# A graph network's max aggregation: eleven tiles taken with one product per pair of source tiles instead of one per source tile

## The chip, the cores and the metric

The kernel runs on one core of one Trainium2 chip. The metric is the device time of one execution in microseconds; the time before is 3248.2 us, the median of three runs (3247.44, 3248.2, 3262.78). Engines are named as the profile names them: PE multiplies matrices, PEld loads its weights, DVE, ACT and POOL are the vector, scalar and GpSimd engines, SP issues most DMAs.

## The reference, cut to what matters

Three layers of a graph network over 6250 nodes and 200,000 edges, sorted by destination. Destinations are drawn as 6250 u² with u uniform, so low-numbered nodes have many edges and high ones few (about 58 a node in tile 3, 33 in tile 11, 24 in tile 21, 20 in tile 30).

```python
def _sage_conv(x, src, dst, Wl, bl, Wr):
    agg = jax.ops.segment_max(x[src], dst, num_segments=x.shape[0])
    agg = jnp.where(jnp.isfinite(agg), agg, 0.0)
    return agg @ Wl + bl + x @ Wr
...
h = jax.nn.leaky_relu(_sage_conv(x, src, dst, Wl1, bl1, Wr1), NEG_SLOPE)
h = jax.nn.leaky_relu(_sage_conv(h, src, dst, Wl2, bl2, Wr2), NEG_SLOPE)
h = jax.nn.leaky_relu(_sage_conv(h, src, dst, Wl3, bl3, Wr3), NEG_SLOPE)
...
h = jnp.maximum(_layernorm(x, axis=-1), 0.0)
x = x + _L0_gnn_ref(h, edge_index, L0_gnn_Wl1, ...)
```

The first layer has 128 features, the second and third 256 on their input side.

## The kernel before, in words

**Tiles.** Nodes are cut into 50 tiles of 127; tile numbers serve for sources and destinations. The 50 source tiles form 25 pairs g. For a tile of destinations and a pair of source tiles, the kernel makes a *one-hot* matrix (in `one_hot`): column d has a one in the row of one source of destination d. The product of the pair's features (`pair_sb`, in two parts whose sum is exact) and the one-hot picks that source's features for all destinations of the tile, and DVE takes the maximum into the accumulator `acc` (`maxima`, L1007). A destination can have several sources in a pair; those that a product does not pick go on a *list* and are fetched row by row.

**Units.** A unit is 128 columns of a one-hot. A *wide* unit ("w") picks one source per source *tile*: two products a pair, each with a maximum of its own. A *narrow* unit ("n") picks one source per *pair*: the products with both source tiles (s = 0 and 1) add up in one PSUM tile `pg`, and one maximum takes it. Both kinds cost PE the same matmuls. Before, tiles 3 to 21 are wide and 22 to 49 narrow; tiles 0 to 2, with the most edges, are spread over eight "virtual" wide units and eight more ("x") that are handled as narrow.

**Groups and sweeps.** Group 0 holds the narrow tiles 30 to 49, group 1 the virtual units, group 2 the wide tiles 3 to 21, group 3 the narrow tiles 22 to 29. A *sweep* runs over all 25 pairs, from the last to the first, for some groups: in layer 0 the groups 0, then 1, then 2 and 3 (called 0a, 0b, 0c here); in layer 1 the groups 0 and 1, then 2 and 3 (1a, 1b); in layer 2 the groups 0 and 1, then 2, then 3 (2a, 2b, 2c). One *step* of the program is one chunk of up to 1024 columns (512 in layers 1 and 2) of one group and pair: eight matmuls of L990 (four where a chunk of layer 0 is at most 512 wide) and one maximum (narrow) or two (wide). There are 225 + 400 + 400 steps.

**Lists.** Each group has a list. `CAPS` gives, for each row of 128 destinations (sorted by how much they have listed), how many gathers it gets; a destination with more than its cap sends the program through a slow fallback behind a branch at the end. The caps sum to 118 + 70 + 230 + 77 = 495 gathers a layer. One gather is an indirect DMA issued by POOL (`Listed.gather`, L1039) that fetches 128 rows of `table` into a quarter (an eighth in layer 0) of a tile `g`; its addresses `let` are copied by ACT from `ell` two steps ahead (`release`, L1028); DVE merges a full `g` into the first (L1053) and folds the result (L1058).

**What sets the order.** The order is written out by hand. `plan(step, rank, f)` puts each gather, release, maximum and node update at a step; gathers are spread evenly over a layer's steps, and their maxima come DELAY = 8, 6, 6 steps later (SOON = 4 for list 3). Each engine runs its own queue in that order, so an engine that is late delays whoever waits for it, and ACT, which makes the one-hots as buffers come free, goes in step with PE.

**Nodes.** When a group is done, `Node` fetches its listed maxima (POOL, L1082), merges them with `acc` (L1098, L1104), does the linear part (L1109 to L1115), and writes the next layer's tables, pairs and transposed rows. The 20 nodes of group 0 and the joined ones of group 1 fall into the first 50 steps of the following sweep, the nodes of groups 2 and 3 into the first 27 steps of the next layer.

**Chores.** The lists and one-hot indices of groups 1 to 3 are made on DVE while layer 0 runs: `flag_rows` finds repeated sources (L488 to L548), `pick_rows` picks what is listed with rounds of MAX8 and MATCH_REPLACE (L558, L560), `rank_rows` sorts, `send_row` scatters by POOL (L624), and `expand` with `lookups` make the index rows (L736 to L769). Group 1's stand in steps 0 to 40, those of groups 2 and 3 in steps 40 to 82. A wide tile needs two look-ups (s = 0 and 1) over 64 columns, a narrow one a single look-up over 40.

Of the kernel before, what the change touches and what calls it, by code (L numbers as in the profile page):

```python
# [36 lines left out]
I16 = mybir.dt.int16  # L37
# [22 lines left out]
)  # L60
NEAR, FIRST = 20, 30
DEEP = (24, 24, 48, 24)
# [7 lines left out]
def kernel(ctx: ExitStack, tc: tile.TileContext, x, src, dst,  # L70
# [31 lines left out]
    PLACE, HEAD = {}, []  # L102
    for units in GROUPS:
        HEAD.append(len(PLACE))
        for u in units:
            PLACE[u] = len(PLACE)
    NU = len(PLACE)
# [4 lines left out]

    TILES = [[tile_of(u) for u in units] for units in GROUPS]
    LISTS = GROUPS
# [30 lines left out]
    IW = [(len(units) + sum(w == "w" for w, _ in units)) * P for units in PLANES]  # L145
# [3 lines left out]
    OW = [sum(w == "w" for w, _ in units) * P for units in PLANES]  # L149
# [400 lines left out]
    def pick_rows(k, i0, us, S):  # L550

        n, W, m = len(us), width_of(us), DEEP[k]
# [10 lines left out]
        nc.vector.tensor_scalar(picked[k][:, i0 : i0 + n, :], top, -float(LEAF), 0.0, op0=OP.add, op1=OP.max)  # L563
        there = S(0, F32, n, m)
        nc.vector.tensor_scalar(there, top, float(LEAF), None, op0=OP.is_ge)
        nc.vector.reduce_sum(left_n[k][:, i0 : i0 + n], there, axis=AX.X)
# [183 lines left out]
    def lookups(us, least, s, pool, tags=("v", "v8")):  # L750
# [9 lines left out]
        while i < n:  # L760
# [9 lines left out]
            at = NV + PLANES[k].index(us[i]) if us[i] in EXTRA else GROUPS[k].index(us[i]) + (len(GROUPS[k]) if s else 0)  # L770
# [61 lines left out]
    for i0 in (0, NEAR // 2):  # L832
        mask_rows(L0[i0 : i0 + NEAR // 2], S_first)
        flag_rows(L0[i0 : i0 + NEAR // 2], S_first)
# [6 lines left out]
        pick_rows(0, i0, L0[i0 : i0 + NEAR // 2], S_first)  # L841
# [88 lines left out]
    def parts_of(k):  # L930

        units = PLANES[k]
        for w in "wnx":
            us = [i for i, u in enumerate(units) if u[0] == w]
            for i0 in range(0, len(us), HOT // P):
                yield us[i0], len(us[i0 : i0 + HOT // P]) * P, len(GROUPS[k]) if w == "w" else 0
# [3 lines left out]
    def one_hot(layer, k, g, c, w, odd, s):  # L940
# [7 lines left out]
        if layer == 0:  # L948
            at = of + (c + (odd if s else 0) + (NV if PLANES[k][c] in EXTRA else 0)) * P
# [27 lines left out]
    def products(step, s, p):  # L977
# [4 lines left out]
        c0, pw, _ = next(q for q in parts_of(k) if q[0] <= c < q[0] + q[1] // P)  # L982
# [82 lines left out]
    class Node:  # L1065
# [28 lines left out]
        def merge(self):  # L1094
# [5 lines left out]
            if self.k is None:  # L1100
# [171 lines left out]
    for layer in range(3):  # L1272
# [7 lines left out]
        for part, t0, t1 in (((lists_[:3], t0, turn), (lists_[3:], turn, t1)) if alone else ((lists_, t0, t1),)):  # L1280
# [3 lines left out]
            n = sum(len(li.seq) for li in part) - early  # L1284
# [6 lines left out]
        done_at, i, at = [], 0, 0  # L1291
        for k, li in enumerate(lists_):
            for t in range(len(li.seq)):
                if whens[i] is None:
                    at = 1 + i // 8
                else:
# [447 lines left out]
```

## Time and profile before

| | us |
|---|---|
| median of three runs | 3248.2 |
| profiled execution, device time | 3258.48 |
| its span, first to last instruction | 3256.5 |

The page has one slice for each fortieth of the span. Its rows on PE, DVE, POOL and the clock:

```profile
PE   1025622448777779999988888889999997878787
DVE  6677899987999987899986799995799897999965
POOL 4787523446777742766664455532466665654563
PEclk9996865678999999999999999999999998999999
```

A digit is the busy share of a slice in tenths; PEclk is the granted clock of TensorE in tenths of full speed. The first three slices are the preparation before the first product. A row of a view by line reads: line, engine, operation, output and input, shapes, count | busy us, mean ns of one | idle us just before them and what ended it. A row of waits reads: who waited, for whom, us in total, times, longest.

### The profile page before, as it was taken

To read this page: it belongs to the slowest core of one execution; us is meant where nothing else is said; L and a number is where in the kernel's file an instruction comes from. 1 tells how busy PE (TensorE), PEld (TensorE's weight loads), DVE (VectorE), ACT (ScalarE), POOL (GpSimd) and SP (SyncE) were. 2 spreads that over 40 slices of the span, in tenths; PEclk is the share of its full clock that TensorE was granted. 3 is DMA by queue.
4 is the path that set the end of the run, shared out by engine and by line. 5 is a ranking of instruction groups with operands and counts; after the bars stand their busy time and mean duration, and the time that the engine had idled before them with its cause. 6 is when DMAs were issued, how large, how long until landed. Compare 5 with 4: busy or idle time off the path is not lost.

```text
span 3256.5 us, 37116 instructions
## 1 busy us (share of the span) xinstructions
PE 2448.4 (75%) x9919; PEld 1785.3 (55%) x9920; DVE 2740.2 (84%) x4320; ACT 1901.7 (58%) x2753; POOL 1862.4 (57%) x1885
## 2 busy tenths in 40 slices
PE   1025622448777779999988888889999997878787
PEld 1023311235444457777765655567777775655566
DVE  6677899987999987899986799995799897999965
ACT  4127942646867656666654566655666664555553
POOL 4787523446777742766664455532466665654563
PEclk9996865678999999999999999999999998999999
DMA  9234521339866767666766655656666575655586
GB/s 305 59 66 139 150 68 33 110 99 242 241 185 194 183 189 230 199 208 201 204 167 192 203 165 177 171 154 212 206 197 203 180 179 181 201 166 159 155 258 182
DMA packets 358250, 571.20 MB, mean 175 GB/s; under 512 B 65270, under 2 KB 213379, under 8 KB 357393
## 3 DMA queue, kind: packets, MB, share of 16 engines
q1 hardware_dynamic: 237201, 341.17, 32.7%
q0 software_dynamic: 77568, 193.35, 23.6%
q10 hardware_dynamic: 43264, 34.21, 3.2%
q8 instruction: 83, 1.36, 0.2%
q14 instruction: 134, 1.10, 0.1%
HBM read 443.95 MB, written 124.54 MB: 175 GB/s over the span
## 4 chain that ended last, share of the span: by engine, by line
PE 36%; DVE 29%; DMA 12%; issue 9%; POOL 5%; ACT 4%; SPq 1%; DVEq 0%; ACTq 0%; POOLq 0%
PE pg L990 28%; DVE acc L1007 13%; POOL g L1039 5%; DMA g<-table,let 4%; PE z_p L1111 3%; DVE g L1058 3%; PE z_p L1113 2%; DVE g L1053 2%; ACT hot L962 2%; ACT away L960 2%; DMA pair_sb<-pair 2%; DVE acc L742 1%; DVE acc L560 1%; DVE acc L558 1%; DVE acc L736 1%
## 5 line engine op out<-in xcount | busy, mean ns | idle before, releaser
L990 PE MATMUL pg<-hot,pair_sb 128*128 128x512 f32 (+1 forms) x8000 | 2150.7, 417 | 411.2 <-ACT hot L962 126.4
L1039 POOL DMA_INDIRECT g<-table,let x1485 | 1510.7, 1017 | 929.1 <-ACT let L1028 359.9
L990 PEld LDWEIGHTS pg<-hot,pair_sb 128*128 128x128 f32 x8000 | 1507.6, 199 | 925.8 <-ACT hot L962 236.8
L1007 DVE TENSOR_TENSOR acc<-acc,pg 128x1024 f32<-128x1024 f32 (+3 forms) x1439 | 1638.3, 1166 | 278.4 <-PE pg L990 251.3
L962 ACT ACTIVATE hot<-away 128x1024 fp32r<-128x1024 uint8 (+2 forms) x600 | 573.9, 957 | 405.8 <-PE pg L990 391.8
L962 ACT ACTIVATE hot<-idx_sb 128x1024 fp32r<-128x1024 uint8 (+2 forms) x600 | 555.0, 937 | 230.3 <-PE pg L990 216.0
L960 ACT ACTIVATE away<-idx_sb,near 128x1024 uint8<-128x1024 uint8 (+2 forms) x600 | 620.4, 1034 | 56.7 <-DMA idx_sb<-idx 25.8
L1082 POOL DMA_INDIRECT agg<-best,end_i x141 | 141.1, 1001 | 236.2 <-PE aT_p L1098 190.6
L1115 ACT COPY s<-z_p 127x256 f32<-127x256 f32 (+1 forms) x150 | 50.3, 335 | 308.1 <-PE z_p L1113 258.4
L1053 DVE TENSOR_TENSOR g<-g 128x1024 f32<-128x1024 f32 (+5 forms) x211 | 206.6, 979 | 10.8 <-DMA g<-table,let 10.7
L1058 DVE TENSOR_TENSOR g<-g 128x256 f32<-128x256 f32 (+3 forms) x357 | 175.5, 492 | 10.6 <-DVE g L1053 0.2
L1111 PE MATMUL z_p<-wr,hT_in 128*128 128x256 f32 (+1 forms) x500 | 136.3, 390 | 1.0 <-DMA hT_in<-across 0.9
L1028 ACT ACTIVATE let<-ell 128x4 int32<-128x4 int16 (+3 forms) x435 | 78.5, 190 | 92.8 <-DMA ell<-picks 82.6
L1113 PE MATMUL z_p<-wl,mz 128*128 128x256 f32 (+1 forms) x500 | 119.7, 356 | 12.2 <-DVE mz L1104 11.4
L624 POOL DMA_INDIRECT picks<-picked,to_i x55 | 56.8, 1032 | 120.9 <-DVE rank_h L600 90.4
L1104 DVE TENSOR_TENSOR mz<-acc,aT_p 128x256 f32<-128x256 f32 (+1 forms) x141 | 52.5, 372 | 72.7 <-PE aT_p L1098 72.7
L956 DVE TENSOR_SCALAR hot<-idx_sb,beyond 128x1024 fp32r<-128x1024 uint8 (+1 forms) x150 | 108.5, 723 | 0.0
L1113 PEld LDWEIGHTS z_p<-wl,mz 128*128 128x128 f32 x500 | 88.6, 203 | 23.8 <-DVE mz L1104 13.8
L1111 PEld LDWEIGHTS z_p<-wr,hT_in 128*128 128x128 f32 x500 | 80.9, 204 | 33.8 <-issue 11.5
L867 ACT COPY hT<-hT_p 128x254 f32<-128x254 f32 x100 | 36.9, 369 | 80.5 <-PE hT_p L865 80.4
L354 POOL DMA_INDIRECT win_d<-in_dst_dram,win_i x50 | 54.2, 1084 | 46.6 <-ACT junk_w L359 18.0
L767 PE MATMUL lk_p<-ident_b,v 128*25 128x128 bf16 x90 | 10.5, 285 | 87.9 <-DVE v L755 59.4
(281 smaller groups left out, 1212.6 us busy)
## 6 DMA issues: line engine op xcount, KB each, us to landing
pair_sb<-pair SPq DMA_DIRECT2D x325, 256.0 KB
idx_sb<-far SPq DMA_DIRECT2D x50, 640.0 KB
far<-away ACTq DMA_DIRECT2D x225, 128.0 KB
pair<-pr SPq DMA_DIRECT2D x100, 256.0 KB
g<-table,let POOLq DMA_INDIRECT x1485
idx_sb<-idx SPq DMA_DIRECT2D x25, 608.0 KB
idx_sb<-far SPq DMA_DIRECT2D x50, 304.0 KB
idx_sb<-idx SPq DMA_DIRECT2D x50, 304.0 KB
```

The source lines that it names most:

```text
L956: nc.vector.tensor_scalar(hot[:, :w], d, beyond, None, op0=OP.is_equal)
L960: nc.scalar.activation(away, d, AF.Abs, bias=near[:, s : s + 1], scale=1.0)
L962: nc.scalar.activation(hot[:, :w], d, AF.Relu, bias=1.0, scale=-1.0)
L990: nc.tensor.matmul(to, pr[:, i, kk * P : (kk + 1) * P], hot[:, o : o + bw], start=((alone or s == 0) and i == 0), stop=((alone or s == 1) ...
L1007: nc.vector.tensor_max(to, to, of)
L1028: nc.scalar.activation(let[:, :n], ell[self.k][:, q, j : j + n], AF.Identity, scale=1.0)
L1039: nc.gpsimd.indirect_dma_start(out=self.tiles[q, b][:, i, :], out_offset=None, in_=tables[self.layer], in_offset=bass.IndirectOffsetOnAxis ...
L1053: nc.vector.tensor_max(base[:, : i + 1, :], base[:, : i + 1, :], g[:, : i + 1, :])
L1058: nc.vector.tensor_max(base[:, :h, :], base[:, :h, :], base[:, w - h : w, :])
L1082: nc.gpsimd.indirect_dma_start(out=self.agg[:, : self.F], out_offset=None, in_=of, in_offset=bass.IndirectOffsetOnAxis(ap=at, axis=0),)
L1111: nc.tensor.matmul(z_p, self.hT[:, i, :], wr[layer][:, i, :], start=False, stop=False)
L1113: nc.tensor.matmul(z_p, self.m[:, i, :], wl[layer][:, i, :], start=False, stop=(i == K - 1))
```

## The change

The border between wide and narrow moves from tile 22 to tile 11: `HI = 11`. Tiles 11 to 21 become narrow: one look-up of 40 columns in place of two of 64, one maximum a pair in place of two, and everything else that their destinations have in a pair is listed. The groups are cut anew: group 2 is the wide tiles 3 to 10 and the narrow tiles 18 to 29 (20 units for 19), group 3 the narrow tiles 11 to 17 (7 for 8). The caps become 118 + 70 + 255 + 110 = 553 gathers a layer. `pick_rows` takes fewer rounds for the narrow tiles of group 2 (32 of 48 places, `NARROWLY`) and the list of group 3 gets 40 places. In layer 2, whose last sweep is group 3 alone, the first 34 gathers of list 3 now come ahead of list 2's, with the usual delay; the other 76 stand in the end as all 77 did. The number of steps is the same, as are matmuls per step but for widths.

```diff
 CAPS = (
     (22, 10, 9, 8, 8, 7, 6, 6, 6, 5, 5, 4, 4, 4, 3, 3, 3, 2, 2, 1),
     (21, 12, 10, 9, 7, 5, 4, 2),
-    (47, 24, 20, 17, 15, 13, 12, 11, 10, 9, 8, 8, 7, 6, 6, 5, 5, 4, 3),
-    (23, 12, 10, 9, 7, 6, 5, 5),
+    (47, 25, 21, 18, 16, 14, 13, 12, 11, 11, 10, 9, 8, 8, 7, 7, 6, 5, 4, 3),
+    (34, 18, 15, 13, 12, 10, 8),
 )
-NEAR, FIRST = 20, 30
-DEEP = (24, 24, 48, 24)
+NEAR, FIRST, MID, HI = 20, 30, 18, 11
+LISTED = 0
+NP = NEAR - LISTED
+DEEP = (24, 24, 48, 40)
+NARROWLY = (24, 0, 32, 40)
...
-    WIDE = list(range(VT, 22))
-    NARROW = list(range(FIRST, NT)) + list(range(22, FIRST))
+    WIDE = list(range(VT, HI))
+    NARROW = list(range(FIRST, NT)) + list(range(MID, FIRST)) + list(range(HI, MID))
     NW, NN = len(WIDE), len(NARROW)
+    BOTH = NEAR + FIRST - MID
     GROUPS = (
-        [("n", i) for i in range(NEAR)],
+        [("n", i) for i in range(NP)],
         [("w", NW + v) for v in range(NV)],
-        [("w", i) for i in range(NW)],
-        [("n", i) for i in range(NEAR, NN)],
+        [("w", i) for i in range(NW)] + [("n", i) for i in range(NEAR, BOTH)],
+        [("n", i) for i in range(BOTH, NN)],
     )
...
     def pick_rows(k, i0, us, S):
 
-        n, W, m = len(us), width_of(us), DEEP[k]
+        n, W, most = len(us), width_of(us), DEEP[k]
+        m = min(most, NARROWLY[k]) if us[0][0] == "n" else most
...
+        if m < most:
+            nc.vector.memset(picked[k][:, i0 : i0 + n, m:], 0)
+            full = S(0, F32, n, 1)[:, :, 0]
+            nc.vector.tensor_scalar(full, left, float(m), float(most - m), op0=OP.is_ge, op1=OP.mult)
+            nc.vector.tensor_add(left, left, full)
...
-        for part in [us]:
+        for part in [list(p) for _, p in itertools.groupby(us, key=lambda u: u[0])]:
             chores.append((2.5, lambda part=part: mask_rows(part, S_acc)))
-            chores.append((18 if part[0][0] == "w" else 6, lambda part=part: flag_rows(part, S_acc)))
+            chores.append((len(part) * (1 if part[0][0] == "w" else .6), lambda part=part: flag_rows(part, S_acc)))
...
-    for i0, i1 in ((0, 7), (7, 13), (13, 19)):
-        for s in range(2):
-            late_lookups(LISTS[2][i0:i1], s)
+    for s in range(2):
+        late_lookups(LISTS[2][:NW], s)
+    rest2 = LISTS[2][NW:]
+    cuts = -(-len(rest2) // 8)
+    for i in range(cuts):
+        late_lookups(rest2[len(rest2) * i // cuts : len(rest2) * (i + 1) // cuts], 0)
...
+        items = [(k, t) for k in range(NL) for t in range(len(lists_[k].seq))]
+        if alone:
+            own = [(3, t) for t in range(len(lists_[3].seq))]
+            later_n = len(items) * (t1 - turn) / (t1 - t0)
+            heads = [t for t, (_, j) in enumerate(lists_[3].seq) if j == 0]
+            cut = min(heads, key=lambda t: abs(len(own) - t - later_n))
+            mid = next(i for i, (k, _) in enumerate(items) if k == 2)
+            items = items[:mid] + own[:cut] + [q for q in items if q[0] == 2] + own[cut:]
+            parted = len(items) - (len(own) - cut)
...
```

DVE's queue in sweep 2b (layer 2, group 2). L1007 is the accumulator maximum, 128x2x512 for a chunk of four units; L1053 and L1058 merge and fold gathered rows. Before, some two pairs:

```order
L1007 TENSOR_TENSOR acc_1513<-acc_1513,pg 128x2x512 x7
L1007 TENSOR_TENSOR acc_1513<-acc_1513,pg 128x2x384 x2
L1007 TENSOR_TENSOR acc_1513<-acc_1513,pg 128x2x512
L1053 TENSOR_TENSOR g<-g 128x1024
L1007 TENSOR_TENSOR acc_1513<-acc_1513,pg 128x2x512 x4
L1053 TENSOR_TENSOR g<-g 128x512
L1058 TENSOR_TENSOR g<-g 128x512
L1058 TENSOR_TENSOR g<-g 128x256
L1007 TENSOR_TENSOR acc_1513<-acc_1513,pg 128x2x512 x3
L1007 TENSOR_TENSOR acc_1513<-acc_1513,pg 128x2x384 x2
```

Now, at the same place (the lines have moved by seven):

```order
L1014 TENSOR_TENSOR acc_1514<-acc_1514,pg 128x2x512 x8
L1060 TENSOR_TENSOR g<-g 128x1024
L1014 TENSOR_TENSOR acc_1514<-acc_1514,pg 128x2x512 x2
L1060 TENSOR_TENSOR g<-g 128x512
L1065 TENSOR_TENSOR g<-g 128x512
L1065 TENSOR_TENSOR g<-g 128x256
L1014 TENSOR_TENSOR acc_1514<-acc_1514,pg 128x2x512 x7
```

A pair had eight 512-wide and two 384-wide maxima; it has seven 512-wide ones. The folds of gathered rows stand closer together.

POOL's queue from sweep 0c over the border of the layers into 1a. L1039 is the gather (table_75 is layer 0's table, table_76 layer 1's), L1082 a node's fetch. Before:

```order
L1039 DMA g<-table_75,let 128x128 x159
L1082 DMA agg<-best_2_142,end_i_852 128x128 x19
L1082 DMA agg<-best_3_143,end_i_853 128x128 x8
L1039 DMA g<-table_76,let 128x256 x252
L1082 DMA agg<-best_0_144,end_i_850 128x256
```

Now:

```order
L1046 DMA g<-table_75,let 128x128 x179
L1089 DMA agg<-best_2_142,end_i_852 128x128 x20
L1089 DMA agg<-best_3_143,end_i_853 128x128 x7
L1046 DMA g<-table_76,let 128x256 x295
L1089 DMA agg<-best_0_144,end_i_850 128x256
```

The same stretch of the program holds 20 more gathers of layer 0 ahead of the border and 43 more of layer 1 behind it; the fetches are 27 as before.

More of the change, by code (lines that the diff above doesn't have):

```diff
@@ L101 @@
     PLANES = [units + (EXTRA if k == 1 else []) for k, units in enumerate(GROUPS)]
[L102 to L107, printed above, removed]
+    LISTS = ([("n", i) for i in range(NEAR)],) + GROUPS[1:]
     def tile_of(u):
@@ L111, in tile_of @@
         return NARROW[i] if w == "n" else WIDE[i] if i < NW else None
-    TILES = [[tile_of(u) for u in units] for units in GROUPS]
-    LISTS = GROUPS
+    TILES = [[tile_of(u) for u in units] for units in LISTS]
     NL = len(LISTS)
@@ L148 @@
     FW = [DW[k] // (2 if k else 1) for k in range(len(GROUPS))]
[L149 removed]
+    OW = [n * P for n in ODD]
     far = [dram.tile([P, NG, FW[k]], U8, name=f"far{k}") for k in range(len(GROUPS))]
@@ L831 @@
     list_consts()
-    for i0 in (0, NEAR // 2):
-        mask_rows(L0[i0 : i0 + NEAR // 2], S_first)
-        flag_rows(L0[i0 : i0 + NEAR // 2], S_first)
+    half = NP // 2
+    for i0, i1 in ((0, half), (half, NP)):
+        mask_rows(L0[i0:i1], S_first)
+        flag_rows(L0[i0:i1], S_first)
         if i0:
@@ L981, in products @@
         K = widths[layer] // P
-        c0, pw, _ = next(q for q in parts_of(k) if q[0] <= c < q[0] + q[1] // P)
+        c0, pw = next(q for q in parts_of(k) if q[0] <= c < q[0] + q[1] // P)
         hot = hots[layer, k, g, c0, s]
@@ L1279 @@
         alone = len(SWEEPS[layer][-1]) == 1
-        for part, t0, t1 in (((lists_[:3], t0, turn), (lists_[3:], turn, t1)) if alone else ((lists_, t0, t1),)):
+        items = [(k, t) for k in range(NL) for t in range(len(lists_[k].seq))]
[7 more added lines that the diff above has]
+            parted = len(items) - (len(own) - cut)
+        for part, t0, t1 in (((items[:parted], t0, turn), (items[parted:], turn, t1)) if alone else ((items, t0, t1),)):
             total = [0.0]
@@ L1283 @@
                 total.append(total[-1] + (WIDER[layer] if steps[t][3][3] is not None else 1.0))
-            n = sum(len(li.seq) for li in part) - early
+            n = len(part) - early
             whens += [None] * early
@@ L1290 @@
                 whens.append(t0 + t)
[L1291 to L1296, printed above, removed]
-                    plan(max(whens[i] - LEAD, 0), LET, lambda li=li, t=t: li.release(t))
-                    plan(whens[i], GATHER, lambda li=li, t=t: li.gather(t))
-                    at = max(at, whens[i] + (SOON if k == NL - 1 else DELAY[layer]))
-                plan(at, MAXIMA, lambda li=li, t=t: li.maximum(t))
-                i += 1
-            done_at.append(at)
+        done_at, at = [0] * NL, 0
+        for i, (k, t) in enumerate(items):
+            li = lists_[k]
+            if whens[i] is None:
+                at = 1 + i // 8
+            else:
+                plan(max(whens[i] - LEAD, 0), LET, lambda li=li, t=t: li.release(t))
+                plan(whens[i], GATHER, lambda li=li, t=t: li.gather(t))
+                at = max(at, whens[i] + (SOON if k == NL - 1 and not (alone and i < parted) else DELAY[layer]))
+            plan(at, MAXIMA, lambda li=li, t=t: li.maximum(t))
+            done_at[k] = at
         gap = (2, 3, 3)[layer]
@@ L1414 @@
     made = making.enter_context(tc.tile_pool(name="made", bufs=1, side="right"))
-    acc_t = [work.tile([P, 2, n * P], F32, name=f"acc{i}") for i, n in enumerate((NN, NV + NW))]
-    ACC = ((0, 0), (1, 0), (1, NV), (0, NEAR))
+    acc_t = [work.tile([P, 2, n * P], F32, name=f"acc{i}") for i, n in enumerate((NP + len(GROUPS[3]), NV + len(GROUPS[2])))]
+    ACC = ((0, 0), (1, 0), (1, NV), (0, NP))
     pair_until(0)
```

34 lines of the change are left out of this document (18 added, 16 removed).

## The prediction

> **What bounds the kernel now.** I read the page first. No engine holds the whole span:
>
> ```profile
> PE 2448.4 (75%) x9919; PEld 1785.3 (55%) x9920; DVE 2740.2 (84%) x4320; ACT 1901.7 (58%) x2753; POOL 1862.4 (57%) x1885
> ```
>
> I read the stages by windows next, then POOL's waits in them, then the groups of instructions by line and shape, and last the timeline at one place. The windows follow the sweeps. Every step issues eight matmuls of L990 (four in the half-width steps of layer 0); counting them in program order in the trace gives the time at which each step starts. The stages below are, from above: steps 40 to 82 (the list chores), the rest of sweep 0b, 0c, 1a from step 275, the first 50 steps of 1b, its other 125, 2a from step 675, the first 50 steps of 2b, its other 75, and 2c.
>
> ```profile
> core 0: us, PE busy (x) PEld busy (x) DVE busy (x) ACT busy (x) POOL busy (x), PEclk, DMA share, GB/s
> 409.00:742.00 333.00, 129.54 (x368) 84.65 (x368) 301.60 (x883) 151.61 (x193) 128.75 (x148) 0.63 0.28 79
> 742.00:899.00 157.00, 123.91 (x485) 82.88 (x485) 136.98 (x179) 115.76 (x171) 111.86 (x107) 0.95 0.90 245
> 899.00:1184.00 285.00, 206.34 (x742) 136.29 (x741) 269.77 (x374) 193.95 (x270) 215.77 (x204) 0.94 0.66 188
> 1330.00:1664.00 334.00, 327.08 (x1396) 258.25 (x1395) 312.27 (x306) 230.02 (x302) 230.95 (x231) 1.00 0.68 200
> 1664.00:1879.00 215.00, 174.05 (x735) 128.47 (x734) 150.21 (x190) 105.15 (x186) 104.67 (x104) 0.92 0.61 188
> 1879.00:2185.00 306.00, 256.10 (x1000) 179.81 (x999) 291.19 (x291) 195.69 (x261) 171.59 (x173) 0.98 0.58 169
> 2349.00:2693.00 344.00, 330.84 (x1401) 261.48 (x1400) 311.81 (x305) 229.79 (x301) 224.33 (x222) 0.99 0.66 194
> 2693.00:2874.00 181.00, 146.22 (x685) 109.64 (x684) 157.59 (x202) 86.87 (x142) 107.63 (x108) 0.92 0.61 183
> 2874.00:3083.00 209.00, 166.38 (x600) 110.97 (x600) 200.25 (x201) 121.62 (x169) 111.57 (x113) 0.94 0.50 155
> 3083.00:3227.00 144.00, 127.86 (x609) 97.79 (x609) 98.06 (x141) 75.09 (x104) 79.39 (x80) 0.96 0.81 245
> ```
>
> In 1a and 2a PE is full (327 of 334 us): 175 steps at 1.91 us. In the late parts of 1b and 2b DVE is (291 of 306, 200 of 209): 2.45 and 2.79 us a step for the same matmuls. The chores are DVE's too (302 of 333). 2c has the DMA at 0.81.
>
> POOL's busy share hides its load. The waits of POOL, in 0c and then in late 1b:
>
> ```profile
> POOL g L1039 <- issue: 46.3, 152, 0.3
> POOL g L1039 <- DMA g<-table,let: 4.6, 15, 0.3
> ```
>
> ```profile
> POOL g L1039 <- ACT let L1028: 53.8, 21, 5.9
> POOL g L1039 <- issue: 36.9, 121, 0.3
> POOL g L1039 <- DVE acc L1007: 23.9, 19, 4.1
> ```
>
> Each gather is followed by 0.3 us in which POOL waits for nothing shown; it cannot be used. In 0c these gaps and the busy time come to 216 + 204 × 0.3 = 277 of 285 us: POOL is full there beside a DVE of 270. In late 1b it has 54 us of waits for the addresses ("let") that ACT hands out two steps ahead, which means that it runs as early as it may.
>
> **The change part by part.** Matmuls, one-hots and steps stay the same in number and all but the same in width: a unit of 128 columns costs PE the same, wide or narrow. Three things change.
>
> (1) *Accumulator maxima, DVE.* Eleven units lose one of two maxima per source pair. Prices, late 1b:
>
> ```profile
> L1007 DVE TENSOR_TENSOR acc<-acc,pg 128x1024 f32<-128x1024 f32 x180 | 212.9, 1216 | 11.8 <-PE pg L990 6.4 <-DVE acc L1007 0.5
> L1007 DVE TENSOR_TENSOR acc<-acc,pg 128x768 f32<-128x768 f32 x34 | 32.3, 950 | 1.6
> ```
>
> That is 1.18 and 0.95 us of DVE each (busy over count). Per source pair 1b goes from ten full and two 768-wide maxima to eight and one: 2 × 1.18 + 0.95 = 3.3 us less. 2b goes from eight and two to seven: 3.1 us less.
>
> (2) *Gathers, POOL,* 58 more a layer, and their maxima on DVE. In 0b and 0c (742 to 1184 us) and then in 1a:
>
> ```profile
> L1039 POOL DMA_INDIRECT g<-table,let x282 | 299.2, 1061 | 88.7 <-issue 67.7 <-DMA g<-table,let 5.8 <-DVE acc L1007 3.0
> ```
>
> ```profile
> L1039 POOL DMA_INDIRECT g<-table,let x228 | 229.7, 1007 | 102.4 <-issue 52.1 <-ACT let L1028 24.5 <-DVE acc L1007 13.7
> L1053 DVE TENSOR_TENSOR g<-g 128x1024 f32<-128x1024 f32 (+3 forms) x39 | 38.7, 993 | 0.0
> L1058 DVE TENSOR_TENSOR g<-g 128x256 f32<-128x256 f32 (+1 forms) x53 | 28.3, 535 | 1.5
> ```
>
> With the gap a gather costs POOL 1.36 us in layer 0 and 1.31 us after, and DVE (38.7 + 28.3) / 228 = 0.29 us.
>
> (3) *The chores, DVE,* steps 40 to 82:
>
> ```profile
> L742 DVE TENSOR_TENSOR acc<-acc 128x960 int16<-128x960 int16 (+6 forms) x100 | 46.9, 469 | 3.4
> L558 DVE MAX8 acc<-acc 128x8 f32<-128x128 f32 (+1 forms) x138 | 37.0, 280 | 4.1
> L736 DVE TENSOR_SCALAR acc<-rows_w 128x384 int16<-128x384 int16 (+1 forms) x150 | 35.6, 303 | 0.3
> L560 DVE MATCH_REPLACE8 acc<-acc,acc 128x128 f32<-128x128 f32 (+1 forms) x111 | 29.5, 265 | 0.0
> L743 DVE TENSOR_REDUCE least<-acc 128x30 int16<-128x240 int16 (+2 forms) x35 | 15.6, 446 | 1.2
> L492 DVE TENSOR_TENSOR acc<-acc 128x1178 int32<-128x1178 int32 (+9 forms) x15 | 13.7, 916 | 0.5
> ```
>
> The look-up tables (L736, L742, L743, 98 us) go from 35 calls to 25 and from 68,800 to 44,600 elements a partition: between 29% and 35% less, I take 32 us. Picking (L558, L560, 66 us) goes from 138 to 131 MAX8 but from 16,100 to 11,500 elements read: 3 to 19 us, I take 12. Flagging (L492 and the lines around it): the wide tiles, which need two such passes, fall from 19 to 8; L492 falls by about 4 us and its neighbours by about as much again, I take 9. The three small instructions added to a narrow pick are nine in all, under 0.25 us each. Sum 53 us of DVE (bounds 38 to 63).
>
> Now the stages, since only the engine that is last there counts:
>
> *Chores, 409 to 742.* DVE is 91% busy, so of 53 us some 46 come off; nothing else is near (POOL has 11 more gathers, 15 us, against 160 idle). Bounds 30 to 58. The cover that could fail: ACT and the DMA, idle here for half the time.
>
> *0b and 0c, 742 to 1184.* 322 instead of 285 gathers are planned between steps 82 and 220: 37 × 1.36 = 50 us on a POOL that has 442 − 327.6 − 311 × 0.3 = 21 us left. The maxima of layer 0 may come eight steps after their gathers, and POOL, waiting for nothing in 0c, has used part of that already; I allow it four more steps, 11 us. DVE's relief here (11 units × 128 columns × 25 at 1.18 us per 1024: 41 us) is worth nothing, as POOL is late. I take +28 (bounds +10 and +50).
>
> *1a and 2a.* 257 gathers instead of 219 in 175 steps: 1a's POOL load goes from 231 + 69 = 300 to 350 us, above the 334 of PE. POOL starts the sweep as early as it may (it waits for "let") and may fall six steps behind before DVE waits, 11 us; so 16 − 11 = 5 us are late, and DVE at 312 + 38 × 0.29 = 323 leaves less room. I take +8 each, +16 (bounds 0 and +45).
>
> *Late 1b.* Eighteen pairs: DVE 291 − 18 × 3.3 + 11 × 0.29 = 235; POOL 172 + 173 × 0.3 + 11 × 1.31 = 238; PE at 1a's pace 125 × 1.88 = 235. Three engines at one mark fill less well than one alone (1a's DVE and POOL stand at 0.93 and 0.90): 237 / 0.93 = 255, so −51. *Late 2b*, fifteen pairs: DVE 200 − 46 + 1 = 155, POOL 145 + 7 = 152, PE 141; 155 / 0.93 = 167, −42. Together −93 (bounds −60 and −106).
>
> *First 50 steps of 1b and 2b.* PE and DVE hand the node updates to each other; DVE has 22 and 30 us less in its queue before them, of which I count less than half: −21 (bounds 0 and −45).
>
> *2c.* Of list 3, whose gathers all stood in these steps, 34 move ahead of list 2's; with the longer list the same 66 gathers are left here, beside seven units for eight and 20 node updates for 19, under a DMA that is the bound: 0 (bounds −5 and +5). *SP and the DMA:* SP issues two transfers fewer in all. The gathers add 58 × (64 + 128 + 128) KB = 19 MB, the narrower index rows of layer 0 take 4 MB away:
>
> ```profile
> DMA packets 358250, 571.20 MB, mean 175 GB/s; under 512 B 65270, under 2 KB 213379, under 8 KB 357393
> ```
>
> Against 571 MB and DMA shares of 0.50 to 0.68 in the stages that change I count that at nothing; in 0b, at 0.90, it is part of the upper bound.
>
> Sum: −46 + 28 + 16 − 93 − 21 = −116. The profiled execution took 3258.5 us (its span 3256.5), 10 above the median of 3248.2; so 3142 on its scale and **3132 us** on that of the median.
>
> A page of the Trainium skill speaks against the exchange. The rows first, DVE and POOL in 1b:
>
> ```profile
> 1666.38 0.95 POOL L1039 DMA_INDIRECT g<-table,let  x1 [0.30 <-issue]
> 1672.36 1.36 POOL L1039 DMA_INDIRECT g<-table,let  x1 [0.31 <-issue]
> ...
> 1666.97 1.21 DVE L1053 TENSOR_TENSOR g<-g 128x1024 f32<-128x1024 f32 x1
> 1671.69 1.22 DVE L1053 TENSOR_TENSOR g<-g 128x1024 f32<-128x1024 f32 x1
> ```
>
> The gather that began before the maximum took 0.95 us, the one that began inside it 1.36. The Trainium skill, "SBUF — State Buffer", section "Who interferes with whom", says that a DVE instruction with two SBUF inputs contends with a GpSimd instruction that reads SBUF, and that the one issued first holds the port. These two rows agree. The change removes maxima with one input in PSUM and adds some with both in SBUF, so by that rule gathers get longer, not shorter; the first rival below gives a time for longer gathers, worked out from rows.
>
> **The rivals.**
>
> *POOL takes the pace (0.16).* Every gather costs layer 0's 1.36 us and the allowance of steps is no use. 0b and 0c: +50; 1a 257 × 1.36 − 334 = +16 and 2a alike +10; late 1b 184 × 1.36 = 250 plus half of the 54 us of waits, −29; late 2b 118 × 1.36 = 160 plus 25, −24; the 50-step parts −10; chores −46. Sum −33: 3215. For it speaks 0c, where POOL already is full; against it the waits in 1b.
>
> *The chores were not what held steps 40 to 82 (0.10),* for instance because the products there wait on one-hots: then −46 goes and layer 0 keeps +50: −48, 3200. DVE at 91% speaks against.
>
> *More is hidden than I allow (0.13):* the better bounds of chores, layer 0 and late 1b and 2b, −58 + 10 − 106, and −25 for the 50-step parts: −179, 3070.
>
> *Slower (0.06).* The waits for "let" stay as long as they are, since ACT writes the addresses behind one-hots that wait for PE; then POOL is one chain and its added work, 50 + 2 × 58 × 1.31 = 202 us, lands whole, while the wide sweeps gain nothing: 202 − 46 = +156, 3404. It decides from where more than about two thirds of the 202 us land. POOL's waits came while it ran early, which speaks against.
>
> *The change does not do what it says (0.03):* the order shows the maxima gone; what is left is a list longer than its cap, which sends the program through the fallback behind the branch at the end, slower by far.
>
> **How the numbers follow.** My forecast has 0.52. What can be told from no change is half a per cent, 16 us. Below 3232 lie the forecast, the case of the chores, the case in which more is hidden, and 0.11 of POOL's: 0.86; within half a per cent 0.05; slower 0.09. The range 3075 to 3225 leaves out the slower cases and the tail below the best one.
>
> **What would show it.** Right: L1007 down from 1439 instructions by about 150; late 1b near 2.04 us a step and late 2b near 2.23, with DVE and POOL about level; 1a and 2a at 1.91 to 2.0; steps 40 to 82 near 290 us; 742 to 1184 longer by 10 to 50. Wrong: POOL without any wait in 1b or 2b, or DVE idle there on "DMA g<-table"; L1039's mean above 1.06 us in layers 1 and 2; the chores' stage unmoved while DVE's busy time in it falls.

## The result, and the profile after

The changed kernel took 3157.3 us (median of four runs, 3153.6 to 3160.6); beside it on the same chip the kernel before took 3255.5 (3247.4 to 3265.5). The ratio is 0.970, with a 95% interval of 0.966 to 0.973. The prediction of 3132 lies 25 us below, its range of 3075 to 3225 holds the result, and faster came true. On another chip the change made the kernel slower; that comes up with the experiments.

The page's row of the engines after the change, and the three groups that answer to L1007, L1039 and L1053:

```profile
PE 2407.1 (76%) x9909; PEld 1806.9 (57%) x9909; DVE 2523.6 (80%) x4059; ACT 1901.4 (60%) x2793; POOL 2049.3 (65%) x2059
...
L1046 POOL DMA_INDIRECT g<-table,let x1659 | 1697.4, 1023 | 677.4 <-issue 383.2
...
L1014 DVE TENSOR_TENSOR acc<-acc,pg 128x1024 f32<-128x1024 f32 (+2 forms) x1239 | 1434.0, 1182 | 296.0 <-PE pg L997 278.9
...
L1060 DVE TENSOR_TENSOR g<-g 128x1024 f32<-128x1024 f32 (+5 forms) x247 | 249.3, 1009 | 63.3 <-DMA g<-table,let 56.3
```

DVE lost 217 us of work, POOL gained 187. The span fell by 101.5. The windows of the changed kernel, cut at the same steps as those of before (steps 40 to 82, the rest of 0b, 0c, 1a from step 275, the first 50 steps of 1b, late 1b, 2a from step 675, the first 50 of 2b, late 2b, 2c):

```profile
core 0: us, PE busy (x) PEld busy (x) DVE busy (x) ACT busy (x) POOL busy (x), PEclk, DMA share, GB/s
416.00:684.00 268.00, 126.13 (x359) 82.17 (x359) 245.41 (x776) 150.10 (x192) 131.97 (x155) 0.67 0.39 98
684.00:834.00 150.00, 122.08 (x483) 83.02 (x483) 135.90 (x183) 115.64 (x175) 116.44 (x111) 0.95 0.89 259
834.00:1162.00 328.00, 213.09 (x739) 155.45 (x738) 239.29 (x328) 194.51 (x274) 248.34 (x242) 0.83 0.60 158
1307.00:1665.00 358.00, 335.75 (x1402) 263.50 (x1400) 323.99 (x321) 231.76 (x315) 274.40 (x266) 0.98 0.69 200
1665.00:1866.00 201.00, 168.18 (x731) 125.54 (x732) 127.94 (x170) 101.17 (x179) 114.16 (x113) 0.93 0.67 207
1866.00:2118.00 252.00, 234.58 (x1004) 183.12 (x1003) 238.11 (x237) 199.51 (x269) 190.48 (x186) 0.99 0.71 212
2281.00:2637.00 356.00, 333.34 (x1399) 260.45 (x1398) 322.72 (x318) 231.09 (x313) 274.30 (x267) 0.99 0.72 204
2637.00:2806.00 169.00, 139.93 (x686) 106.81 (x685) 129.83 (x175) 89.52 (x143) 116.73 (x115) 0.94 0.67 203
2806.00:2974.00 168.00, 149.16 (x604) 112.02 (x603) 156.85 (x157) 123.49 (x170) 121.71 (x121) 0.98 0.64 199
2974.00:3117.00 143.00, 122.43 (x621) 99.27 (x619) 91.19 (x138) 68.98 (x104) 83.23 (x81) 0.94 0.82 243
```

Add 0.3 us for the gap behind each instruction to POOL's busy time, and POOL's load comes to 248 + 73 = 321 of 328 us in 0c, to 274 + 80 = 354 of 358 in 1a and of 356 in 2a. It is full in all three. POOL's own waits in 1a, and then DVE's, say the same:

```profile
POOL g L1046 <- issue: 62.2, 204, 0.3
```

```profile
DVE acc L1014 <- PE pg L997: 17.8, 32, 1.7
DVE g L1060 <- DMA g<-table,let: 10.5, 5, 4.4
```

POOL has its fixed gaps and next to nothing else, and five times DVE stands for gathered rows that are not there yet. In 0c that costs more:

```profile
DVE g L1060 <- DMA g<-table,let: 34.5, 7, 10.5
```

The lengths of the stages, from one step's first matmul to another's, on the chips where the first comparison and the runs e5, e6, g1 and g2 were made:

```
stage (us)                before  after  g1 pace  g2 trim  e5 twice  e6 half
steps 40 to 82             333.0  268.2    273.0    271.3     306.0    269.8
82 to 125 (rest of 0b)     156.8  150.0    157.7    156.6     143.1    149.8
0c                         284.8  328.8    293.4    276.7     328.3    328.0
1a from step 275           335.3  358.0    342.9    344.8     359.7    336.8
first 50 steps of 1b       214.3  201.0    206.4    198.7     200.2    195.9
late 1b                    306.7  251.4    248.9    254.3     252.8    243.0
2a from step 675           344.1  356.6    342.3    345.2     355.7    337.6
first 50 steps of 2b       181.3  169.2    182.6    161.2     172.1    165.8
late 2b                    209.0  167.4    163.3    161.0     167.3    157.1
2c                         143.6  143.5    145.2    143.7     143.6    134.4
span                      3256.5 3155.0   3114.2   3061.8    3188.4   3078.6
```

What the change gains it gains where DVE was the last (steps 40 to 82, 1b, 2b: −187 us); what it gives back it gives back where POOL is (0b and 0c, 1a, 2a: +72). The rest is +13, 8 of it behind the last product.

### The profile page after: what moved, and what is told of

It reads as the page before. It is cut to its first block, busy times and chain, and to the rows that moved or that the text cites. A ratio compares the mean times of both kernels' runs of the same rounds, so it can differ in the third digit from the quotient of the medians.

```text
span 3155.0 us, 36991 instructions
## 1 busy us (share of the span) xinstructions
PE 2407.1 (76%) x9909; PEld 1806.9 (57%) x9909; DVE 2523.6 (80%) x4059; ACT 1901.4 (60%) x2793; POOL 2049.3 (65%) x2059
## 3 DMA queue, kind: packets, MB, share of 16 engines
q8 instruction: 83, 1.36, 0.2%
q14 instruction: 135, 1.11, 0.1%
## 4 chain that ended last, share of the span: by engine, by line
PE 33%; DVE 26%; DMA 16%; issue 9%; POOL 7%; ACT 5%; SPq 1%; DVEq 0%; ACTq 0%; POOLq 0%
PE pg L997 25%; DVE acc L1014 11%; DMA g<-table,let 8%; POOL g L1046 6%; PE z_p L1118 3%; DVE g L1065 3%; DVE g L1060 3%; ACT away L967 2%; PE z_p L1120 2%; ACT hot L969 2%; DMA pair_sb<-pair 1%; DVE acc L560 1%; DMA hT_in<-across 1%; DVE acc L558 1%; PE hT_p L872 1%
## 5 line engine op out<-in xcount | busy, mean ns | idle before, releaser
L997 PE MATMUL pg<-hot,pair_sb 128*128 128x512 f32 x8000 | 2113.5, 416 | 383.0 <-DVE acc L1014 108.0
L1046 POOL DMA_INDIRECT g<-table,let x1659 | 1697.4, 1023 | 677.4 <-issue 383.2
L997 PEld LDWEIGHTS pg<-hot,pair_sb 128*128 128x128 f32 x8000 | 1532.9, 200 | 834.9 <-ACT hot L969 229.9
L1014 DVE TENSOR_TENSOR acc<-acc,pg 128x1024 f32<-128x1024 f32 (+2 forms) x1239 | 1434.0, 1182 | 296.0 <-PE pg L997 278.9
L1060 DVE TENSOR_TENSOR g<-g 128x1024 f32<-128x1024 f32 (+5 forms) x247 | 249.3, 1009 | 63.3 <-DMA g<-table,let 56.3
L1065 DVE TENSOR_TENSOR g<-g 128x256 f32<-128x256 f32 (+3 forms) x357 | 176.9, 496 | 10.5
L1035 ACT ACTIVATE let<-ell 128x4 int32<-128x4 int16 (+3 forms) x477 | 86.5, 189 | 103.2 <-DMA ell<-picks 92.5
L963 DVE TENSOR_SCALAR hot<-idx_sb,beyond 128x1024 fp32r<-128x1024 uint8 (+2 forms) x150 | 108.8, 725 | 0.0
L1105 PE MATMUL aT_p<-ident,agg 128*128 128x128 f32 x250 | 54.4, 284 | 22.7 <-DMA agg<-best,end_i 14.2
```

What stands on the lines that cost most here:

```text
L963: nc.vector.tensor_scalar(hot[:, :w], d, beyond, None, op0=OP.is_equal)
L997: nc.tensor.matmul(to, pr[:, i, kk * P : (kk + 1) * P], hot[:, o : o + bw], start=((alone or s == 0) and i == 0), stop=((alone or s == 1) ...
L1014: nc.vector.tensor_max(to, to, of)
L1035: nc.scalar.activation(let[:, :n], ell[self.k][:, q, j : j + n], AF.Identity, scale=1.0)
L1046: nc.gpsimd.indirect_dma_start(out=self.tiles[q, b][:, i, :], out_offset=None, in_=tables[self.layer], in_offset=bass.IndirectOffsetOnAxis ...
L1060: nc.vector.tensor_max(base[:, : i + 1, :], base[:, : i + 1, :], g[:, : i + 1, :])
```

## The experiments

**Theories.** Mine: DVE's time sets steps 40 to 82; the 58 added gathers a layer, through POOL, are what made 0c, 1a and 2a longer. Rivals: the new grouping of look-ups and lists made them longer; the bytes of the gathered rows did; a gather costs as much wherever it stands.

**A second kind of chip.** e1 to e4 ran on one chip and f1 to f4 on another, and both are slower: the kernel before takes 3566.1 and 3571.9 us there, and 3255.5, 3258.1 and 3259.2 on those of the first comparison, of e5 and e6, and of g1 and g2. The chips of the experiments were each used at one time only, so a lasting property of a chip and a passing one can't be told apart; "kind" stands for either. Ratios are to the kernel before on the same chip. The programs of e5, e6 and f4 were measured once each. What is different on the second kind is told at the end of this section.

**e1, f2, g2: the changed kernel with 495 gathers a layer.** The rows past these lists are left out.

```diff
+GETS = CAPS[:2] + (
+    (47, 24, 20, 17, 15, 13, 12, 11, 10, 9, 8, 8, 7, 6, 6, 5, 5, 4, 2, 1),
+    (23, 13, 11, 9, 8, 7, 6),
+)
...
-            self.seq = [(q, j) for q, m in enumerate(CAPS[k]) for j in range(m)]
+            self.seq = [(q, j) for q, m in enumerate(GETS[k]) for j in range(m)]
...
```

> The changed kernel with 495 gathers a layer again (lists 2 and 3 are cut to 230 and 77 gathers; the rest of what is listed is left out, so some maxima miss sources). If POOL's rate sets the pace of 0c, 1a and 2a in the changed kernel: 0c goes from 329 to 270-285 us, 1a (from step 275) from 358 to about 335, 2a from 357 to about 344, late 1b and 2b by under 10 us each, the whole from 3157 to about 3065. If the longer sweeps come from the regrouped order and not from the gathers: 0c, 1a and 2a stay as they are, 3145 to 3157.

> The changed kernel with its lists cut to the 495 gathers a layer of the kernel before (rows past that are left out). Theory, that POOL's added gathers cost what 0c, 1a and 2a gained in length: 0c back to 285 to 295 us, 1a and 2a to 333 to 342, the late parts of 1b and 2b shorter by 5 to 15 each, some 95 us in all off the changed kernel. Rival, that the new grouping of look-ups and lists made these stages longer and not the number of gathers: 0c stays above 315, 1a and 2a above 350.

> The changed kernel with the 495 gathers a layer of the kernel before, once more (rows past the shorter lists are left out). On a chip on which the kernel before takes some 3570 us: 0.96 to 0.97 of it. On one on which it takes some 3255 us: by the theory that the added gathers made 0c, 1a and 2a longer, 0c at 285 to 295, 1a and 2a at 333 to 342, late 1b and 2b 5 to 15 shorter each, 3050 to 3080 in all; by the rival, that the new grouping did, 0c above 315 and 1a and 2a above 350, 3130 or more.

On the first kind of chip (g2) it took 3062.6 us, 0.940 (0.938 to 0.942) of the kernel before. Its windows of 0c, 1a and late 1b:

```profile
839.40:1116.20 276.80, 198.30 (x742) 142.76 (x742) 231.34 (x322) 193.26 (x271) 210.97 (x204) 0.91 0.62 178
1260.40:1605.20 344.80, 327.98 (x1401) 258.84 (x1400) 316.78 (x310) 230.71 (x306) 246.51 (x244) 1.00 0.70 200
...
1803.90:2058.20 254.30, 236.37 (x1001) 185.14 (x999) 231.71 (x234) 197.51 (x263) 168.34 (x167) 0.98 0.64 199
```

The rival of the grouping is out: 0c falls to 277, not above 315. The exchange without its price is worth 3259 − 3063 = 196 us, and the 174 added gathers cost 3157 − 3063 = 95, or 0.54 each: 1.11 in 0b and 0c (45.5 us for 41), 0.55 in 1a (13.2 us for 24) and 0.35 in 2a (11.4 us for 33 planned), nothing in late 1b, which takes 254 us for 251 though 19 instructions fewer stand on POOL. There DVE and PE, both at 0.91 to 0.93, hold the pace, as the prediction had it. My expectation of 5 to 15 us less missed there; late 2b, at 161 for 167, met it. 0c fell further than I expected (285 to 295), and 1a and 2a less far (333 to 342): both stay at 345. In 1a only 13 of the +23 us go with the gathers. With them gone it is not back at before's 335: the new groups deal the same 495 otherwise, 242 into 1a for 227. Whether that is all of the 10 us, or the new grouping has another part in it, is open. On the second kind the same kernel took 3449.1 (e1, 0.966) and 3447.9 us (f2, 0.965).

**e2: the kernel before with 553 gathers a layer.** It alone has the price without the gain.

```diff
-    (47, 24, 20, 17, 15, 13, 12, 11, 10, 9, 8, 8, 7, 6, 6, 5, 5, 4, 3),
+    (47, 28, 25, 22, 20, 18, 17, 15, 14, 12, 11, 10, 9, 8, 8, 7, 6, 6, 5),
```

> The kernel before, with 58 more gathers a layer, all in list 2, which fetch the floor row and change nothing in the result: the gathers of the change without its maxima and chores. If POOL's rate is the price: 0c +40 to +50 us, 1a and 2a +10 to +25 each, late 1b and 2b, where DVE is the bound and POOL has 64 and 61 us of waits, at most +10 each; the whole +75 to +105, about 3345. If gathers hide beside PE and DVE: +0 to +20.

It ran on the second kind alone: 3744.9 us, 1.049 (1.043 to 1.056). That is 1.03 us for each of 174 gathers. The stage lengths that were expected hold for the first kind and can't be compared.

**f1: the changed kernel on the second kind of chip.**

> The changed kernel once more, as the measure for the three that run beside it on the same chip: near 0.97 of the kernel before. If the gain found at first belongs to one chip only, then above 0.985.

It took 3655.4 us, 1.023 (1.017 to 1.028) of the kernel before: slower than before, though the interval does not clear 2%. Against f2 on the same chip, the added gathers cost 207 us there, 1.19 each; maxima and chores gain 124.

**e3, f3, g1: the same gathers dealt out otherwise.** A weight on the steps in which POOL idles; e3 had 1.8 in layer 0 and 1.5 after, f3 and g1 as shown.

```diff
+    def pace(layer, t):
+        t0, n, much = (ends_at[layer, 1], 46, (0, 1.2, 1.4)[layer]) if layer else (52, 32, 1.5)
+        return much if t0 <= t < t0 + n else 1.0
...
-                total.append(total[-1] + (WIDER[layer] if steps[t][3][3] is not None else 1.0))
+                total.append(total[-1] + pace(layer, t) * (WIDER[layer] if steps[t][3][3] is not None else 1.0))
```

> The changed kernel with the same gathers at other steps: weights 1.8 on steps 52 to 83 in layer 0 and 1.5 on the first 46 steps of 1b and 2b, so that 0c has some 25 gathers fewer and 1a and 2a some 15 fewer. If POOL's rate is what holds 0c, 1a and 2a: 0c from 329 to about 295, 1a and 2a from 358 and 357 to about 340 each, the chores' stage and the 50-step parts up by at most 10 each: about 3105. If the landing of the gathers' data or DVE holds them: 0c, 1a and 2a within 10 us of the changed kernel, 3145 to 3165.

> The same 553 gathers, dealt out otherwise: 26 more of them in steps 40 to 82 and 15 fewer in 0c; 7 fewer in 1a and 12 more in the first 50 steps of 1b; 14 fewer in 2a and 22 more in the first 50 of 2b. Theory, that POOL is full in 0c, 1a and 2a and idle in the other three: 0c shorter by 20 us, 1a by 9, 2a by 16, late 2b by 6, the other stages as they are; some 50 off the changed kernel. Rival, that a gather costs about as much where POOL is idle because DVE and the node updates wait for it: steps 40 to 82 longer by 20 or more, the first 50 steps of 1b by 10 and of 2b by 20, and the whole within 15 of the changed kernel.

> The kernel with its gathers dealt out otherwise, once more. If the chip is one on which the kernel before takes some 3570 us (there engines were seen to wait for each other until POOL's run of gathers ended): 1.02 to 1.035 of the kernel before, as the changed kernel itself there. If it is one on which the kernel before takes some 3255 us: by the theory that POOL is full in 0c, 1a and 2a alone, 0c near 309 us, 1a near 349, 2a near 340, the other stages as in the changed kernel, 3100 to 3115 in all; by the rival, that a gather costs as much in the stages where POOL idles, 3145 or more, with steps 40 to 82 at 285 or above and the first 50 steps of 1b and 2b at 211 and 189 or above.

On the first kind (g1) it took 3114.5 us, 0.955 (0.954 to 0.957) of the kernel before: 43 less than the changed kernel on the chip of the first comparison, and less than both kernels. Steps 40 to 82, 0c, 1a and the first 50 of 1b:

```profile
412.70:685.70 273.00, 130.85 (x359) 85.17 (x359) 249.62 (x782) 151.12 (x201) 153.93 (x180) 0.63 0.45 104
...
843.40:1136.70 293.30, 204.01 (x741) 147.28 (x740) 233.27 (x319) 192.85 (x269) 224.16 (x216) 0.86 0.64 170
1283.70:1626.60 342.90, 330.43 (x1401) 259.72 (x1401) 321.19 (x317) 231.41 (x312) 261.74 (x259) 1.00 0.71 206
1626.60:1833.10 206.50, 168.26 (x733) 125.17 (x732) 131.84 (x175) 101.77 (x184) 127.09 (x125) 0.93 0.68 209
```

In steps 40 to 82, 26 more gathers cost 5 us; from step 82 to the end of 0c, 20 fewer save 28, or 1.39 each, which is one gather and its gap. 1a with 7 fewer saves 15 and 2a with 14 fewer 14. In 1a the mean gather is shorter too, 1.011 us for 1.033, so POOL's load falls by 14 us, to 262 + 78 = 340 of 343: just at the bound. The first 50 steps of 1b take 5 us more for 12 more gathers and those of 2b 13 us more for 22, so the last part of the shift buys little. The rival of equal prices is out on this kind of chip. On the second kind the shift is worth nothing: 1.025 (e3) and 1.029 (f3) of the kernel before, beside 1.023 for the changed kernel.

**e4: maxima of gathered rows four steps later,** `DELAY = (12, 10, 10)` for (8, 6, 6).

> The changed kernel with the gathered rows' maxima four steps later (DELAY 12, 10, 10). If POOL's rate is the pace, the allowance is used up once in each of 0c, 1a and 2a: 8 to 12 us less in each, not more, POOL full as before: 3125 to 3140. If it is the time that a gather's data takes to land after POOL has issued it, four steps (8 us) cover it: 1a and 2a go to 335 and 344, 0c to 285, about 3080.

It ran on the second kind alone, 3701.6 us, 1.037 (1.032 to 1.042). The changed kernel was not run on that chip; on the other chip of this kind it was at 1.023, so this says only that the delay shows no help there; whether more slack would help in 0c on the first kind is open.

**e5: the look-ups of the narrow tiles in steps 40 to 82 made twice.** The second pass writes what the first wrote.

```diff
-                expand(us, CB if us[0][0] == "n" else CUT, g0, s, got[0], S_acc)
+                for _ in range(2 if us[0][0] == "n" else 1):
+                    expand(us, CB if us[0][0] == "n" else CUT, g0, s, got[0], S_acc)
```

> The changed kernel with the look-ups of its narrow late units made twice (15 more calls of expand, each five L742, two L748 and one L749, about 2.5 us of DVE by the rows of the changed kernel: some 38 us). If DVE holds steps 40 to 82, the stage goes from 268 to about 302 us (295 to 310). If ACT, POOL or the DMA holds it: within 8 us of 268.

```profile
413.70:719.80 306.10, 129.45 (x359) 83.22 (x359) 279.46 (x898) 150.20 (x192) 137.98 (x163) 0.65 0.36 89
```

DVE has 34 us more (279.5 for 245.4), the stage 38 (306.1 for 268.1). So DVE holds these steps, and a microsecond of its work is worth slightly more than one in the stage: the stage's idle time goes along. But the steps behind, 82 to 125, take 143 us for 150, and the whole, 3190.3 us, is 33 above the changed kernel for 34 of work: while DVE is busy longer POOL gets ahead, with 163 instructions in the stage for 155.

**e6: half rows.** In layers 1 and 2 a gather fetches a row of 128 features, from layer 0's table, and not one of 256. Eight of them fit in a tile `g`, for four, so DVE has less to do over them (47 us for 80 in 1a). What the rows of layers 1 and 2 would have given is left out.

```diff
-            self.F = widths[layer]
+            self.F = D
...
-                out=self.tiles[q, b][:, i, :], out_offset=None, in_=tables[self.layer],
+                out=self.tiles[q, b][:, i, :], out_offset=None, in_=tables[0],
...
```

> The changed kernel in which layers 1 and 2 gather rows of 128 instead of 256 features, from layer 0's table (so the listed part of their maxima is not computed): as many gathers, half their bytes, half their DVE work. If POOL's issue is the pace of 1a and 2a: both stay within 8 us of 358 and 357. If the gathers' bytes, their landing or DVE hold them: 335 to 344.

**f4: full rows, half maxima.** Gathers as in the changed kernel; DVE takes the maxima over 128 of the 256 features, and the others are left out.

```diff
-                nc.vector.tensor_max(base[:, : i + 1, :], base[:, : i + 1, :], g[:, : i + 1, :])
+                nc.vector.tensor_max(base[:, : i + 1, :D], base[:, : i + 1, :D], g[:, : i + 1, :D])
...
-                    nc.vector.tensor_max(base[:, :h, :], base[:, :h, :], base[:, w - h : w, :])
+                    nc.vector.tensor_max(base[:, :h, :D], base[:, :h, :D], base[:, w - h : w, :D])
```

> Gathers as in the changed kernel, full rows; DVE's maxima over gathered rows take 128 of a row's 256 features in layers 1 and 2 (the others are left out). Theory, that gathers are lengthened by DVE's maxima with both inputs in SBUF, and that DVE's time for them counts: 1a and 2a at 337 to 345 us as with half rows, the mean gather in them at 0.97 to 0.99 us. Rival, that the bytes of the rows (or when they land) set 1a and 2a: both at 352 to 359, the mean gather at 1.02 or above.

e6 took 3080.4 us. 1a fell to 337 and 2a to 338, so the expectation that as many instructions on POOL mean the same time failed. The group of gathers in 1a comes first after the change, then in e6; behind it stand e6's window of 1a and the only waits of DVE in it:

```profile
L1046 POOL DMA_INDIRECT g<-table,let x266 | 274.6, 1033 | 83.7 <-issue 62.2 <-DMA g<-table,let 7.8 <-DVE acc L1014 7.3
```

```profile
L1046 POOL DMA_INDIRECT g<-table,let x265 | 257.1, 970 | 81.1 <-issue 59.1 <-DMA g<-table,let 9.2 <-ACT hot L969 4.6
```

```profile
1307.50:1644.30 336.80, 326.13 (x1401) 259.10 (x1400) 295.82 (x310) 230.75 (x315) 256.04 (x265) 1.00 0.61 162
```

```profile
DVE acc L1014 <- PE pg L997: 34.4, 63, 0.6
```

A gather is shorter by 0.063 us. POOL's load, 265 × (0.970 + 0.3) = 337 us, still is the length of the stage, but DVE waits for gathered rows no more, only for PE, and PE is busy for 326 of 337 us, as it was for 327 of 334 before the change. So the shorter gathers, or DVE's smaller work, took away what POOL was late by; whether POOL or PE holds what is left of the stage, e6 doesn't tell. Are the gathers shorter for the bytes? The same row in f1 and in f4, which ran on one chip:

```profile
L1046 POOL DMA_INDIRECT g<-table,let x265 | 271.5, 1025 | 151.9 <-issue 67.2 <-ACT let L1035 64.5 <-DVE acc L1014 14.0
```

```profile
L1046 POOL DMA_INDIRECT g<-table,let x263 | 256.1, 974 | 169.5 <-issue 69.9 <-ACT let L1035 50.4 <-DVE acc L1014 40.3
```

With all the bytes and 48 us of DVE's work over gathered rows for 80, the gather takes 0.974 for 1.025. So it is DVE's maxima with both inputs in SBUF that make gathers longer, and not the rows' size: this half of f4's theory is shown. The single gathers say it too. In 1a of the changed kernel 45 took over 1 us, and every one of them began while DVE ran one of L1060 and L1065; the 164 that met none of these took 0.95. The other half of that theory, that DVE's time for the maxima counts for the length of the stage, could not be seen, since f4 (3687.8 us) fell on the second kind of chip, where 1a takes 422 us for f1's 423. The Trainium skill, "SBUF — State Buffer", section "Who interferes with whom", has a DVE instruction with two SBUF inputs contend with a GpSimd instruction that reads SBUF; the four rows agree with it, as a gather takes its addresses from `let` in SBUF.

**What the second kind of chip does.** Most instructions are as long there: the mean gather is 1.019 us in f1 for 1.023, L1014 1.184 for 1.182. PE's matmuls of L997 take 0.432 us for 0.416, at a granted clock of 0.87 for 0.91, and PE is busy for 138 us more; the span is 500 us longer. What is longer above all is the time between instructions. DVE's longest waits in f1, over the whole span:

```profile
DVE acc L1014 <- PE pg L997: 395.0, 309, 9.4
DVE acc L1014 <- remote: 228.3, 63, 21.0
```

"remote" is a release to which the trace shows no finished instruction. One place in 1a, all engines:

```profile
1486.72 1.22 DVE L1014 TENSOR_TENSOR acc<-acc,pg 128x1024 f32<-128x1024 f32 x1 [2.34 <-PE pg L997]
...
1488.08 1.17 PE L997 MATMUL pg<-hot,pair_sb 128*128 128x512 f32 x4 [0.98 <-DVE acc L1014]
1488.38 0.95 POOL L1046 DMA_INDIRECT g<-table,let  x1 [0.30 <-issue]
...
1497.14 0.94 POOL L1046 DMA_INDIRECT g<-table,let  x1 [0.30 <-issue]
1498.39 0.95 POOL L1046 DMA_INDIRECT g<-table,let  x1 [0.30 <-issue]
1499.35 1.22 DVE L1014 TENSOR_TENSOR acc<-acc,pg 128x1024 f32<-128x1024 f32 x1 [11.41 <-remote]
1500.69 1.35 PEld L997 LDWEIGHTS pg<-hot,pair_sb 128*128 128x128 f32 x4 [11.87 <-issue]
```

PE's four matmuls are done by 1489.3, and DVE waits for nothing else. POOL gives out nine gathers on end, the last one done at 1499.34; then, at 1499.35, DVE starts. The trace records when a semaphore, the counter by which one engine tells the others that it is done, is raised: for this matmul at 1499.33. For every instruction that raises its engine's semaphore I took the time from its end to the next update that is recorded:

```
                      DVE's updates       PE's updates      of the late ones, inside a run of
                      over 1 us late      over 1 us late    POOL's indirect DMAs (gaps < 0.4 us)
before, first kind      2 of 3731           2 of 2467
after, first kind       1 of 3518           0 of 2404
g1, first kind          0 of 3522           3 of 2404
f1, second kind       889 of 3518         704 of 2404       92% and 94%
f2, second kind       817 of 3469         679 of 2404       89% and 93%
e2, second kind       951 of 3772         718 of 2467       90% and 94%
```

In f1 an update of DVE is late in 35% of the cases inside such a run and in 6% outside. These counts are upper bounds: f1 has only 2354 records for DVE's 3518 updates, the changed kernel on the first kind 3516, and an update without a record of its own counts as late when the next one comes. The starts of instructions don't depend on these records. Of DVE's 1275 instructions that take a product, 153 start in f1 over 1 us after the product and DVE's work before are done, and none in the same program's trace on the first kind; 91% of the 153 fall into runs of gathers, which hold 74% of all 1275. So on these chips engines start late on each other's results, and more often while POOL runs gathers back to back. That would make a gather dear where POOL is not the bound, and 1.03 us (e2) and 1.19 us (f2 against f1) for each added one fit. But it is read from traces; no run put pauses between gathers to try it, and what makes these chips differ is open.

## Why the prediction was right

The path was the one forecast, with a chance of 0.52: DVE sheds time where it is the bound, POOL takes on more where it is or becomes it. Against the profiled execution's 3258.5 the sum was −116; measured are 3156.75, −102. Term by term, forecast and measured:

```
chores                        -46     -65
0b and 0c                     +28     +37
1a and 2a                     +16     +35
late 1b and late 2b           -93     -97
first 50 steps of 1b and 2b   -21     -25
2c                              0       0
all else                        0     +13
```

The mechanism held, but that the sum came so close is in part luck: three terms came out 41 us dearer than forecast (0b and 0c, 1a and 2a, all else) and three 27 us cheaper. The other 10 of the 25 us are the 10 by which the profiled execution before lay above its median; after the change it lies on it. Of "all else", put at nothing, 8 us lie behind the last product: 38 us for 30 before, and 30 again in g2.

*Chores.* The mechanism held, as e5 shows; the size was off. DVE's work fell by 56 us, 3 more than summed, and the stage by 65: I let 46 of 53 us count, but the waits within the stage shrank with it (333 − 302 = 31 us without DVE before, 23 after). In e5 7 of 38 us come back in the steps behind, so part of what was gained here beyond the forecast is likely to be what 0b and 0c lost.

*0b and 0c.* The bound was POOL's load, 37 × 1.36 = 50 us, less the room that was left and four more steps of slack. g2 and g1 measure 1.11 and 1.39 us a gather here: the load was sized well, the slack was too generous. When 0c begins, 19 gathers whose addresses ACT has released still stand before POOL, 6 before the change: it is late there already.

*1a and 2a.* This step failed in size. POOL's load was forecast at 350 us for 1a and was 354 (266 gathers in the trace for my 257, but 227 for my 219 before); but I let 11 us of it be absorbed because POOL entered the sweep early. After the change it enters with no lead: 12 gathers with released addresses stand before POOL as 1a begins, 5 before the change, and it waits for addresses 1 us in all, for 24.5 before. Gathers also grew, from 1.008 to 1.033 us in 1a and from 1.009 to 1.031 in 2a, 266 × 0.025 = 7 and 266 × 0.022 = 6 us. In these stages and in 0c the first rival, POOL takes the pace (+16, +10 and +50), was as near as my forecast, while its late 1b and 2b (−29 and −24) were far off. The sign that I had named for it, POOL without waits in 1b, did come:

```profile
POOL g L1046 <- issue: 40.5, 133, 0.3
POOL g L1046 <- DVE acc L1014: 7.0, 23, 0.3
```

Every wait is of the fixed 0.3 us; late 1b has POOL at 190 + 56 = 246 of 252, and yet g2 shows that the stage is no faster with fewer gathers. Engines at one mark do not say which one holds.

*Late 1b and 2b.* −55 and −42 for −51 and −42; 2.01 and 2.23 us a step for 2.04 and 2.23. The filling of 0.93 was nearly right: DVE is busy for 0.94 and 0.93.

*Signs.* L1014 has 200 instructions fewer than L1007 had, not 150: I had left out the 50 of layer 0, whose time counts for nothing since POOL is late there. The gather's mean stayed below 1.06 us in layers 1 and 2, as the forecast had it.

*The rule of the Trainium skill* that spoke against the change was right in sign: gathers grew. By the rows it is worth 7 and 6 us in 1a and 2a. With its gap a gather takes 1.33 us there, between the 1.31 of the forecast and the 1.36 of the rival that priced longer gathers.

*What it could not see.* Nothing in the profile of before told that on another chip the change would cost 2.3% (1.7 to 2.8). "Slower" was priced there by waits for addresses; what the traces there show is another thing, engines that start late on each other's results.

## What to carry to other kernels

An engine's load is its busy time and its fixed gaps: POOL at 77% busy was full, and a stage with a full engine pays each added instruction at its whole price, while the same instruction costs 0.2 to 0.6 us in a stage where the engine idles (g1), for 1.3 where it is full. So when work moves from one engine to another, place the added work stage by stage where the receiver idles; that was worth 43 us here beyond the change itself, on the first kind of chip. A gain that rests on one engine's slack should be measured on more than one chip.

## What the hardware showed unexpectedly

- A gather of 128 rows lasts 0.97 us beside little and 1.03 beside much DVE work with two inputs in SBUF, whether its rows are 512 or 1024 bytes long.
- On two of the chips the kernel before takes 9.5% and 9.7% longer, and 174 gathers cost 207 us for 95. In f1 153 of DVE's 1275 instructions that take a product start over 1 us late, where the same program on another chip has none, and a third of DVE's semaphore updates has no record of its own.
- The gap behind a gather that waits for nothing was 0.3 us in every trace read here, on both kinds of chip.
